# Token tiles by feature through VectorE's block transposes and DRAM in a one-core DiT block

## The chip, the core and the metric

The kernel runs on one core of one Trainium2 chip. The metric is the device time in microseconds of one execution; lower is better. The core has a matrix engine (TensorE, PE in the profile, with its weight loads as PEld), VectorE (DVE), ScalarE (ACT), GpSimd (POOL), and SyncE (SP), which here only issues DMAs. Each engine works through its own queue in order; the engines wait for one another by semaphores.

## The reference

One block of a diffusion transformer in float32: B = 2 sequences of N = 2048 tokens, C = 576 features, H = 16 heads of 36, an MLP of 2304. Cut to what matters:

```python
mod = silu(c) @ w_ada + b_ada          # 6 rows of C per sequence
sh1, sc1, g1, sh2, sc2, g2 = split(mod, 6)
xn = ln(x, 1e-6) * (1 + sc1) + sh1
q, k, v = split(xn @ w_qkv + b_qkv)    # (B, N, H, 36) each
q, k = ln(q, 1e-5, qn_g, qn_b), ln(k, 1e-5, kn_g, kn_b)
o = softmax(q @ k.T / 6) @ v
x = x + g1 * (o @ w_proj + b_proj)
xn2 = ln(x, 1e-6) * (1 + sc2) + sh2
out = x + g2 * (gelu(xn2 @ w1 + b1) @ w2 + b2)
```

A matmul on PE needs the features, over which it sums, on the partitions. Tokens are normed with a token on each partition, because the mean and variance are over its features. So every tile of 128 tokens has to be turned from tokens on partitions to features on partitions, twice in the block: ahead of the q/k/v products and ahead of the MLP's first product. The modulation by `sc` and `sh` is applied after turning, where scale and shift are one number for each partition.

## The kernel before

The branch that runs is `block_of_small`. It does everything in one program with these stages, in this order: the adaptive rows; for each sequence, the q/k/v products of 16 token tiles (`inputs`), attention (`attend`) and the projection (`outputs`); then the MLP over all tokens.

576 features are four chunks of 128 and a last one of 64. A turned tile has the last 64 features twice, on partitions 0 to 63 and 64 to 127: `rows_normed` copies columns 512:576 behind the row (L280), so that a fifth PE transpose of 128 columns yields both copies.

*q/k/v.* In `inputs`, a tile has three products (q, k, v) of 576 outputs, each as two halves of 288 columns. `whole` (L400) does the four full chunks as float32 matmuls; `halved` (L411) does the last 64 features as a matmul on half of the array's rows, partitions 0 to 63 for one half of the columns and 64 to 127 for the other. Turning is by `transposed`: four PE transposes at L357, one at L358, into PSUM. ACT then modulates from PSUM to SBUF (`modulated`, L365, five instructions). The turned tile of t+1 is made during tile t, between its q and k products; the norm of t+2 follows. VectorE evicts the products with their bias (`biased`), centres the heads of q and k, and turned heads go through nine PE transposes (L938). For the first two tiles of all, x is loaded ahead, and the first tile of batch 0 is turned with the adaptive rows.

*Projection.* `outputs(b)` does o times w_proj with the residual in groups of four tiles. VectorE multiplies the product by the gate (L1183) and adds x (L1190); POOL's queue loads the residual's rows (L1178) and stores them (L1191). A dictionary `between` hangs further work on certain tiles: in batch 0's projection the first tile of batch 1; in batch 1's the norm, transposes and modulation of the MLP's first five tiles, and the eight `weight_sums` on VectorE, of which four split the MLP's last 64 weight rows, wr, into float32r parts (`weight_parts`, L394 and L395, with L1358).

*MLP.* The first product is a scheme of seven products for four blocks of weights and tokens, in 72 jobs: eight blocks of 512 tokens, nine jobs to a block. Float32 matmuls at L1445 do the 512 full features, and float32r matmuls at L1459 the last 64. [...] the rows are split into a rounded part and what is left, and their products are summed. `last_modulated` (L382, L383) makes two ACT outputs of the last features, a float32r one in `parts` and a float32 one in `tail`; POOL subtracts them (L384). `gelu_stored` evicts each job: ACT copies one part out of PSUM (L1471), VectorE does four sums (L1472 to L1479), ACT the gelus (L1483), SP's queue the stores. `ahead(job)` prepares the next block's four tiles: x is loaded by POOL's queue three jobs early, normed one job early, turned by four PE transposes one job later and by the fifth two jobs later (L1505), and modulated (L1515).

*What sets the order.* PE's order follows the program text. VectorE's order is written by hand (`manual_schedule`) in `inputs`, in `attend`, and from batch 1's projection through the MLP; the other queues are ordered by a planner, so a queue can take an instruction ahead of another where the text has it later. A tile pool with `bufs=1` has one buffer for a name: the next writer waits for the last reader.

## Time and profile before

| | us |
|---|---|
| median of 3 runs | 3216.81 (3216.06 to 3217.01) |
| profiled execution | 3216.58 |
| its span in the profile | 3214.8 |
| PE busy | 3192.7 |
| ACT busy | 1509.1 |
| VectorE busy | 1459.6 |
| POOL busy | 369.1 |
| q/k/v of batch 0, of batch 1 | about 18.9 to 258, 1109.7 to 1347 |
| attention of batch 0, of batch 1 | to 1037.7, to 2120.85 |
| projection of batch 0, of batch 1 | to 1109.7, to 2199.98 |
| MLP's first product, second product | to 2719.28, to 3213 |

The mean granted clock of TensorE is 0.999 of full speed. The stages are read from PE's timeline in microseconds from the span's start; each is given by its end where it begins at the end of the one before. The profiled execution is 1.8 us longer than its span, which covers the core's instructions alone.

In a group's line, "out<-in" names the tiles that an instruction writes and reads, then come its shape, its count, its busy time and the mean length of one in nanoseconds, and last the idle time of its engine just before it with what ended that. Matmuls overlap one another, so a mean length is longer than what one matmul takes of PE. A float32 matmul has two records, a float32r matmul one.

### The profile page before, as it was taken

What the parts mean: (1) busy time and instruction counts of PE and PEld (TensorE: products, weight loads), DVE (VectorE), ACT (ScalarE), POOL (GpSimd) and SP (SyncE); (2) the same over time, 40 slices, a digit from 0 to 9 for tenths busy, and PEclk for the clock granted to TensorE, in tenths of its full rate; (3) what the DMA queues carried; (4) which work ended last, traced back from release to release, by engine and by line L of the source; (5) the groups of instructions that cost most, each with busy time, mean ns of one, the idle gap of its engine ahead of it and who ended that gap; (6) DMA issues with size and microseconds to landing.
All of it is one profiled execution on the core that took longest, in us unless ns stands there. A gap on an engine that the chain in (4) does not pass through costs nothing.

```text
span 3214.8 us, 47053 instructions
## 1 busy us (share of the span) xinstructions
PE 3192.7 (99%) x18143; PEld 1904.6 (59%) x18143; DVE 1459.6 (45%) x2137; ACT 1509.1 (47%) x2984; POOL 369.1 (11%) x464
## 2 busy tenths in 40 slices
PE   8999999999999999999999999999999999999999
PEld 6774333333333777633333333358888888777777
DVE  4674333333333367633333333345555444455454
ACT  2335666666666033466666666633555552000000
POOL 2111000112110111200001111011000000111111
PEclk9999999999999999999999999999999999999999
DMA  4102212223221401121222223144322223333321
GB/s 132 30 26 68 75 33 69 64 72 86 71 81 34 145 23 31 30 54 44 48 47 67 65 69 75 44 160 166 121 88 91 95 80 128 136 133 111 118 103 38
DMA packets 129172, 252.86 MB, mean 79 GB/s; under 512 B 22947, under 2 KB 68460, under 8 KB 126828
## 3 DMA queue, kind: packets, MB, share of 16 engines
q1 hardware_dynamic: 105428, 181.78, 18.6%
q0 software_dynamic: 22640, 66.23, 7.4%
q8 instruction: 145, 2.38, 0.3%
q10 hardware_dynamic: 872, 1.77, 0.2%
q14 instruction: 87, 0.71, 0.1%
HBM read 135.11 MB, written 66.35 MB: 63 GB/s over the span
## 4 chain that ended last, share of the span: by engine, by line
PE 98%; DMA 1%; DVE 0%; SPq 0%; issue 0%; ACT 0%; POOL 0%; DVEq 0%; POOLq 0%
PE b L1086 28%; PE b L1073 19%; PE s L1610 15%; PE s L400 15%; PE m L1445 12%; PE m L1459 2%; PE s L411 2%; PE one L1445 2%; PE s L938 1%; PE s L357 0%; PE t L1505 0%; DMA wq<-in_w_qkv_dram 0%; DMA x_dram<-x 0%; PE b L192 0%; PE b L938 0%
## 5 line engine op out<-in xcount | busy, mean ns | idle before, releaser
L1077 ACT ACTIVATE pt<-b 128x512 f32<-128x512 f32 x2048 | 1057.7, 610 | 485.3 <-PE b L1086 272.2
L1086 PE MATMUL b<-pt,vt 128*64 128x512 f32 x4096 | 935.0, 599 | 0.0
L1086 PEld LDWEIGHTS b<-pt,vt 128*64 128x64 f32 x4096 | 272.0, 136 | 581.8 <-issue 439.2
L1073 PE MATMUL b<-qm,km 32*128 32x512 f32 x4096 | 566.9, 614 | 0.2 <-DMA km<-qo 0.2
L1134 DVE TENSOR_TENSOR ot<-b,ot 128x512 f32<-128x512 f32 x192 | 132.8, 692 | 652.9 <-PE b L1086 652.5
L1073 PE MATMUL b<-qe,ke 16*128 16x512 f32 x2048 | 423.1, 790 | 0.0
L400 PE MATMUL s<-wq,xnt 128*128 128x288 f32 x1536 | 391.4, 409 | 1.2 <-ACT xnt L882 0.8
L1610 PE MATMUL s<-ws,as 128*128 128x288 f32 x1440 | 351.8, 406 | 0.0
L1073 PEld LDWEIGHTS b<-qm,km 32*128 32x128 f32 x4096 | 191.8, 185 | 269.1 <-ACT pt L1077 207.0
L400 PEld LDWEIGHTS s<-wq,xnt 128*128 128x128 f32 x1536 | 285.1, 190 | 85.4 <-issue 13.5
L1610 PEld LDWEIGHTS s<-ws,as 128*128 128x128 f32 x1440 | 274.1, 190 | 75.1
L1105 DVE RECIPROCAL den<-den 128x512 f32<-128x512 f32 x64 | 213.6, 3337 | 10.8 <-DMA den<-den_dram 10.8
L1445 PE MATMUL m<-s,wb 128*128 128x256 f32 x864 | 210.1, 380 | 0.2 <-DVE s L1415 0.2
L1445 PE MATMUL m<-xnt,wb 128*128 128x256 f32 x864 | 210.2, 379 | 0.0
L1132 DVE COPY ot<-b 128x512 f32<-128x512 f32 x64 | 44.3, 692 | 334.7 <-PE b L1086 334.7
L1445 PEld LDWEIGHTS m<-s,wb 128*128 128x128 f32 x864 | 164.4, 190 | 22.5 <-DVE s L1415 0.6
L1073 PEld LDWEIGHTS b<-qe,ke 16*128 16x128 f32 x2048 | 108.3, 184 | 114.2 <-issue 112.8
L1445 PEld LDWEIGHTS m<-xnt,wb 128*128 128x128 f32 x864 | 159.1, 190 | 18.7
L1472 DVE TENSOR_TENSOR cs<-m,cs 128x512 f32<-128x512 f32 x72 | 49.8, 691 | 215.8 <-PE m L1459 207.1
L1610 PE MATMUL s<-ws,hidden 128*128 128x288 f32 x576 | 142.3, 406 | 0.0
L1588 DVE TENSOR_TENSOR as<-hidden 128x1152 f32<-128x1152 f32 x80 | 139.2, 1803 | 0.0
L400 PE MATMUL s<-wp,qo 128*128 128x288 f32 x512 | 127.8, 410 | 0.0
(182 smaller groups left out, 2573.9 us busy)
## 6 DMA issues: line engine op xcount, KB each, us to landing
gelu<-cs SPq DMA_DIRECT2D x144, 256.0 KB
hidden<-gelu SPq DMA_DIRECT2D x16, 2304.0 KB
den<-den_dram SPq DMA_DIRECT2D x128, 128.0 KB
x_dram<-kr POOLq DMA_DIRECT2D x48, 288.0 KB, 2.8
qm<-qo SPq DMA_DIRECT2D x192, 64.0 KB
kr<-in_x_dram POOLq DMA_DIRECT2D x32, 288.0 KB, 3.8
xr<-x_dram SPq DMA_DIRECT2D x32, 288.0 KB
out_dram<-y POOLq DMA_DIRECT2D x30, 288.0 KB, 3.8
```

What stands on the lines that cost most here:

```text
L400: nc.tensor.matmul(outs[a], stationary(k, a), moving(k, a), start=(first and k == 0), stop=(not first and k == FULL - 1),)
L411: nc.tensor.matmul(outs[a], stationary(FULL, a)[r], moving(FULL, a)[r], start=first, stop=not first)
L1073: nc.tensor.matmul(ps, k[r, keys], q[r, :], start=first, stop=not first)
L1077: nc.scalar.activation(pt[:, h, :], banks[2 * c + h], AF.Exp, scale=SCALE)
L1086: nc.tensor.matmul(acc[64 * h : 64 * h + 64, :], vt[:, v0 : v0 + 64], pt[:, h, :], start=pt is pts[0][0], stop=pt is pts[-1][0],)
L1105: nc.vector.reciprocal(den, den)
L1134: nc.vector.tensor_tensor(ot, acc, ot, ALU.add)
L1445: nc.tensor.matmul(out_m[m], wb[:, slot[m], k, f * P : (f + 1) * P], moving[m](k), start=k == 0 and m in (1, 2, 5, 6), stop=k == 1 and m == 1,
L1459: nc.tensor.matmul(out_m[m], wr[w][:, f * P : (f + 1) * P], a[:, i, t * PAIR : (t + 1) * PAIR], start=False, stop=i == 1 and m != 2,)
L1472: nc.vector.tensor_tensor(cs[:, 0:5:4, :], two(1), cs[:, 4:5, :].to_broadcast([P, 2, PAIR]), ALU.add)
L1588: nc.vector.tensor_tensor(stationary[m], x_, y_, op)
L1610: nc.tensor.matmul(ms[m], stationary[m][:, f, :], ws[m][:, f, :], start=(f == 0), stop=(f == HF - 1))
```

## The change

Turned tiles no longer come from PE. VectorE transposes the normed tile in blocks of 32x32 into a tile `squares` (one buffer). Four DMAs write it to DRAM with runs of 32 numbers, 128 bytes, so that DRAM holds the tile with features as rows (`tile_turned`). Three DMAs read it back with features on partitions: the four full chunks into `xnt`, the last 64 features twice into `tail` (`turned_loaded`). ACT modulates in place (`turned_modulated`). The first tile and, as `second_by_feature`, the second tile of batch 0 are still turned by PE.

The q/k/v products no longer use `halved`: the last 64 features of a tile are split into float32r parts as the MLP's are, and so are the last 64 rows of w_qkv, by `weight_parts` on VectorE, which come through the tile `bq` before the bias is loaded into it. For each half of the columns, two float32r matmuls take the place of the halved one, for 12 instead of 6 of a tile's matmuls.

The splitting of the MLP's last weight rows goes from VectorE to POOL (`last_parts`). In the MLP x is loaded four jobs ahead, normed and written two jobs ahead, read back at the job and modulated at the next. The DMAs go by SP's queue in `inputs` and in the MLP, and by ACT's in the two projections.

```diff
@@ -266,7 +266,7 @@
-    def rows_normed(pool, xt):
+    def rows_normed(pool, xt, repeated=True):
@@ -277,7 +277,8 @@
-        nc.scalar.copy(xt[:, C:], xt[:, 512:576])
+        if repeated:
+            nc.scalar.copy(xt[:, C:], xt[:, 512:576])
@@ -373,6 +374,14 @@
+    def part_tiles(pool, cols, **bufs):
+        return (
+            pool.tile([P, FULL, cols], F32, name="xnt", **bufs),
+            pool.tile([P, 2, cols], F32R, name="xnt4", **bufs),
+            pool.tile([P, P], F32, name="tail", bufs=1),
+        )
     def affine(which, k, b):
@@ -385,14 +394,17 @@
     def modulated_parts(dst, cols, t4, t1, which, b):
-        last_modulated(dst, cols, t1, which, b)
...
-    def weight_parts(dst, src):
-        nc.vector.tensor_copy(dst[0:64], src)
-        nc.vector.tensor_tensor(dst[64:128], src, dst[0:64].bitcast(F32), ALU.subtract)
+        last_modulated(dst, cols, t1, which, b)
+    def weight_parts(dst, src, subtract=None):
+        if subtract is None:
+            nc.vector.tensor_copy(dst[0:64], src)
+        else:
+            subtract.tensor_copy(dst[0:64], src)
+        (subtract or nc.vector).tensor_tensor(dst[64:128], src, dst[0:64].bitcast(F32), ALU.subtract)
     def whole(outs, stationary, moving, first):
@@ -748,13 +760,13 @@
-        def token_tiles(count):
+        def token_tiles(count, width=C):
             pool, close = opened("xs", side="right")
-            more = [pool.tile([P, C + 64], F32, name=f"xt{i}") for i in range(count - 1)]
+            more = [pool.tile([P, width], F32, name=f"xt{i}") for i in range(count - 1)]
...
-        close_xs = token_tiles(5)
+        close_xs = token_tiles(3, C + 64)
@@ -846,13 +858,14 @@
         def input_weights(then=lambda t: None):
...
-            wq4 = pool.tile([P, 3, HALF], F32, name="wq4")
+            wq4 = pool.tile([P, 3 * C], F32R, name="wq4")
...
-                    last_chunk(wq4, w_qkv, 3, HALF)
+                    nc.sync.dma_start(out=bq[0:64, :], in_=w_qkv[512:576, :])
+                    weight_parts(wq4, bq[0:64, :])
@@ -868,27 +881,61 @@
         def tile_normed(xt):
...
-        def input_rows(b, t, queue):
-            return tile_normed(tile_loaded(x[b, t * P : (t + 1) * P, :], queue))
-        def input_by_feature(b, rows, apart=False):
-            xnt = xs["pool"].tile([P, NKC, P], F32, name="xnt", bufs=2)
-            modulated(xnt, rows, 0, b, apart)
+        SQ = 32
+        def tile_turned(xt, queue):
+            rows_normed(xs["pool"], xt, repeated=False)
+            squares = xs["pool"].tile([P, C], F32, name="squares", bufs=1)
+            nc.vector.transpose(squares, xt[:, :C])
+            xs["count"] = xs.get("count", 0) + 1
+            turned = dram.tile([C, P], F32, name=f"turned{xs['count']}")
+            by_square = turned.rearrange("(k d) (g j) -> g d k j", d=SQ, j=SQ)
+            for g in range(P // SQ):
+                queue.dma_start(
+                    out=by_square[g], in_=squares[g * SQ : (g + 1) * SQ, :].rearrange("p (k j) -> p k j", j=SQ)
+                )
+            return turned
+        def turned_loaded(dst, cols, turned, queue):
+            full, _, tail = dst
+            queue.dma_start(out=full[:, :, cols], in_=turned[0:512, :].rearrange("(k p) n -> p k n", p=P))
+            for r0 in (0, 64):
+                queue.dma_start(out=tail[r0 : r0 + 64, :], in_=turned[512:576, :])
+        def turned_modulated(dst, cols, which, b):
+            full, _, tail = dst
+            for k in range(FULL):
+                part = full[:, k, cols]
+                nc.scalar.activation(part, part, AF.Identity, **affine(which, k, b))
+            last_modulated(dst, cols, tail, which, b)
+        def input_turned(b, t, queue):
+            return tile_turned(tile_loaded(x[b, t * P : (t + 1) * P, :], queue), queue)
+        def input_loaded(turned, queue):
+            xnt = part_tiles(xs["pool"], P, bufs=2)
+            turned_loaded(xnt, slice(0, P), turned, queue)
...
+        def input_modulated(b, xnt):
+            turned_modulated(xnt, slice(0, P), 0, b)
+            return xnt
+        def second_by_feature(rows):
+            xnt = part_tiles(xs["pool"], P, bufs=2)
+            t4, t1 = transposed(*rows, True)
+            modulated_parts(xnt, slice(0, P), t4, t1[:, :P], 0, 0)
+            return xnt
         def first_modulated():
...
+            xnt = part_tiles(xs["pool"], P, bufs=2)
+            modulated_parts(xnt, slice(0, P), x_first[:, :512], x_first[:, 512:], 0, 0)
...
-        def inputs(b, weights, work, xnt, loaded):
+        def inputs(b, weights, work, xnt, rows, loaded):
@@ -965,18 +1012,20 @@
             def next_rows(t):
-                return tile_normed(loaded.pop(0)) if loaded else input_rows(b, t, nc.sync)
+                return tile_turned(loaded.pop(0), nc.sync) if loaded else input_turned(b, t, nc.sync)
             def product(w, xnt):
...
...
+                full, parts, _ = xnt
+                for a in range(2):
+                    f = slice(w * C + a * HALF, w * C + (a + 1) * HALF)
+                    out_a = ps[:, a, :HALF]
+                    for k in range(FULL):
+                        nc.tensor.matmul(out_a, full[:, k, :], wq[:, k, f], start=k == 0, stop=False)
+                    for i in range(2):
+                        nc.tensor.matmul(out_a, parts[:, i, :], wq4[:, f], start=False, stop=i == 1)
+                return ps
             def biased(w, ps, t, both):
@@ -991,34 +1040,28 @@
-            rows = next_rows(1)
+            if b == 0:
+                rows = tile_normed(loaded.pop(0))
...
-                q, q_parts = product(0, xnt)
-                whole(*q_parts, True)
-                behind = b == t == 0
-                if behind:
-                    k, k_parts = product(1, xnt)
-                    whole(*k_parts, True)
-                ahead = input_by_feature(b, rows, t in ((0, 9), (0, 1))[b])
+                turning = b == t == 0
+                if not turning:
+                    ahead = input_loaded(rows, nc.sync)
+                q = product(0, xnt)
+                k = product(1, xnt)
+                if turning:
+                    ahead = second_by_feature(rows)
+                else:
+                    input_modulated(b, ahead)
                 rows = next_rows(t + 2)
-                if not behind:
-                    k, k_parts = product(1, xnt)
-                    whole(*k_parts, True)
-                v, v_parts = product(2, xnt)
-                halved(*q_parts, False)
-                halved(*k_parts, False)
-                halved(*v_parts, True)
...
-                whole(*v_parts, False)
+                v = product(2, xnt)
@@ -1028,16 +1071,17 @@
+                if t + 1 < NT:
+                    ahead = input_loaded(rows, nc.sync)
                 for w in range(3):
-                    ps, parts = product(w, xnt)
-                    two_products(*parts, 3 * t + w)
+                    ps = product(w, xnt)
...
-                            ahead = input_by_feature(b, rows)
+                            input_modulated(b, ahead)
@@ -1294,11 +1338,13 @@
-                    9: [lambda: opening.update(rows=input_rows(b + 1, 0, nc.scalar))],
-                    14: [lambda: opening.update(xnt=input_by_feature(b + 1, opening["rows"]))],
+                    6: [lambda: opening.update(rows=input_turned(b + 1, 0, nc.scalar))],
+                    8: [lambda: opening.update(xnt=input_loaded(opening["rows"], nc.scalar))],
+                    10: [lambda: opening.update(rows=input_turned(b + 1, 1, nc.scalar))],
+                    12: [lambda: input_modulated(b + 1, opening["xnt"])],
...
-                xnt = opening["xnt"]
+                xnt, rows = opening["xnt"], opening["rows"]
@@ -1352,11 +1398,14 @@
+        left, right = last_rows[:, 0], last_rows[:, 1]
+        last_parts = [
+            lambda: weight_parts(wr[0], left, nc.gpsimd),
+            lambda: weight_parts(wr[1], right, nc.gpsimd),
+            lambda: nc.gpsimd.tensor_tensor(right, right, left, ALU.subtract),
+            lambda: weight_parts(wr[2], right, nc.gpsimd),
+        ]
         weight_sums = [
-            lambda: weight_parts(wr[0], last_rows[:, 0]),
-            lambda: weight_parts(wr[1], last_rows[:, 1]),
-            lambda: nc.vector.tensor_tensor(last_rows[:, 1], last_rows[:, 1], last_rows[:, 0], ALU.subtract),
-            lambda: weight_parts(wr[2], last_rows[:, 1]),
@@ -1368,22 +1417,23 @@
-        def block_modulated(to, i, turned, b):
-            t4, t1 = turned
-            modulated_parts(to, slice(i * P, (i + 1) * P), t4, t1[:, :P], 2, b)
...
-            between.setdefault(2 * j + 6, []).append(
-                lambda j=j, n=n, i=i: block_modulated(xnts[n], i, transposed(*first[j]), 0)
+            cols = slice(i * P, (i + 1) * P)
+            between.setdefault(2 * j + 6, []).append(lambda n=n, cols=cols: turned_modulated(xnts[n], cols, 2, 0))
+            between.setdefault(2 * j + 1, []).append(
+                lambda j=j, n=n, i=i: first.update({j: mlp_loaded(n, i, nc.scalar)})
...
-                lambda j=j, n=n, i=i: first.update({j: mlp_loaded(n, i, nc.scalar)})
+                lambda j=j: first.update({j: tile_turned(first[j], nc.scalar)})
             )
-            between.setdefault(2 * j + 5, []).append(lambda j=j: first.update({j: tile_normed(first[j])}))
-        for i, t in enumerate((6, 7, 8, 9, 10, 11, 12, 14)):
+            between.setdefault(2 * j + 4, []).append(
+                lambda j=j, n=n, cols=cols: turned_loaded(xnts[n], cols, first[j], nc.scalar)
+            )
+        for i, t in enumerate((6, 8, 10, 12)):
             between.setdefault(t, []).append(weight_sums[i])
+            between.setdefault(t + 1, []).append(last_parts[i])
@@ -1493,32 +1542,18 @@
-            if todo := at(-3):
+            if todo := at(-4):
                 rows_ahead[todo] = mlp_loaded(*todo, nc.gpsimd)
-            if todo := at(-1):
-                rows_ahead[todo] = tile_normed(rows_ahead[todo])
-            for offset, chunks in ((1, range(FULL)), (2, (FULL,))):
+            if todo := at(-2):
+                rows_ahead[todo] = tile_turned(rows_ahead[todo], nc.sync)
+            for offset in (0, 1):
...
-                    src, tail = rows_ahead[todo] if offset == 1 else rows_ahead.pop(todo)
...
+                    cols = slice(i * P, (i + 1) * P)
+                    if offset == 0:
+                        turned_loaded(xnts[m % 2], cols, rows_ahead.pop(todo), nc.sync)
+                    else:
+                        turned_modulated(xnts[m % 2], cols, 2, m // NBLK)
```

More of the change, by code (lines that the diff above doesn't have):

```diff
@@ L877, in input_by_feature @@
             return xnt
         def first_modulated():
-            xnt = xs["pool"].tile([P, NKC, P], F32, name="xnt", bufs=2)
-            for k in range(NKC):
-                nc.scalar.activation(
-                    xnt[:, k, :],
-                    x_first[:, k * P : (k + 1) * P],
-                    AF.Identity,
-                    bias=mod[:, 0, k, 0:1],
-                    scale=mod[:, 1, k, 0:1],
-                )
+            xnt = part_tiles(xs["pool"], P, bufs=2)
+            modulated_parts(xnt, slice(0, P), x_first[:, :512], x_first[:, 512:], 0, 0)
@@ L967, in next_rows @@
             def next_rows(t):
-                return tile_normed(loaded.pop(0)) if loaded else input_rows(b, t, nc.sync)
+                return tile_turned(loaded.pop(0), nc.sync) if loaded else input_turned(b, t, nc.sync)
             def product(w, xnt):
                 ps = s_tile()
-                return ps, (
-                    [ps[:, a, :HALF] for a in range(2)],
-                    lambda k, a: xnt[:, k, :],
-                    lambda k, a: (
-                        wq[:, k, w * C + a * HALF : w * C + (a + 1) * HALF] if k < FULL else wq4[:, w, :]
-                    ),
-                )
+                full, parts, _ = xnt
[7 more added lines that the diff above has]
+                return ps
             def biased(w, ps, t, both):
@@ L1230, in block_of_small @@
         xnt = first_modulated()
-        loaded = []
+        rows, loaded = None, []
         weights, close_weights = input_weights(
@@ L1237, in block_of_small @@
             with tc.manual_schedule(engines={mybir.EngineType.DVE}):
-                last_inputs = inputs(b, weights, work, xnt, loaded)
+                last_inputs = inputs(b, weights, work, xnt, rows, loaded)
             close_weights()
@@ L1409, in block_of_small @@
         ps_m1 = banks.tile([P, 2, PAIR], F32, name="one")
-        ps_t = banks.tile([P, 512], F32, name="t")
         def token_sums(n):
@@ L1494, in at @@
                 return (m + 1, g // 2) if there else None
-            if todo := at(-3):
+            if todo := at(-4):
                 rows_ahead[todo] = mlp_loaded(*todo, nc.gpsimd)
-            if todo := at(-1):
-                rows_ahead[todo] = tile_normed(rows_ahead[todo])
-            for offset, chunks in ((1, range(FULL)), (2, (FULL,))):
+            if todo := at(-2):
+                rows_ahead[todo] = tile_turned(rows_ahead[todo], nc.sync)
+            for offset in (0, 1):
                 if todo := at(offset):
                     m, i = todo
-                    src, tail = rows_ahead[todo] if offset == 1 else rows_ahead.pop(todo)
-                    for k in chunks:
-                        nc.tensor.transpose(
-                            ps_t[:, k % FULL * P : (k % FULL + 1) * P],
-                            src[:, k * P : (k + 1) * P] if k < FULL else tail,
-                            ident,
-                        )
-                    block = xnts[m % 2]
-                    if offset == 2:
-                        last_modulated(block, slice(i * P, (i + 1) * P), ps_t[:, :P], 2, m // NBLK)
-                        continue
-                    for k in chunks:
-                        nc.scalar.activation(
-                            block[0][:, k, i * P : (i + 1) * P],
-                            ps_t[:, k * P : (k + 1) * P],
-                            AF.Identity,
-                            bias=mod[:, 2, k, m // NBLK : m // NBLK + 1],
-                            scale=mod[:, 3, k, m // NBLK : m // NBLK + 1],
-                        )
+                    cols = slice(i * P, (i + 1) * P)
[3 more added lines that the diff above has]
+                        turned_modulated(xnts[m % 2], cols, 2, m // NBLK)
         for m, k, n in ((2, 0, 0), (5, 1, 1), (3, 0, 1), (4, 1, 0)):
```

## The prediction

> **What bounds the kernel now.** I read the page's first and fourth parts, then PE's groups by shape, then PE's timeline over one q/k/v tile and over the second projection. On the page:
>
> ```profile
> PE 3192.7 (99%) x18143; PEld 1904.6 (59%) x18143; DVE 1459.6 (45%) x2137; ACT 1509.1 (47%) x2984; POOL 369.1 (11%) x464
> PE 98%; DMA 1%; DVE 0%; SPq 0%; issue 0%; ACT 0%; POOL 0%; DVEq 0%; POOLq 0%
> ```
>
> PE is 99% of the span and 98% of the chain, the other engines under half. An instruction taken from PE is worth its whole slot; one put elsewhere costs only if PE comes to wait for it. PE's groups that the change touches (out<-in, shapes, count | busy us, mean ns | idle before):
>
> ```profile
> L400 PE MATMUL s<-wq,xnt 128*128 128x288 f32 x1536 | 391.4, 409 | 1.2 <-ACT xnt L882 0.8 <-DMA wq<-in_w_qkv_dram 0.4
> L1459 PE MATMUL m<-parts,wr 128*128 128x256 f32 x576 | 91.0, 301 | 0.0
> L411 PE MATMUL s<-wq,xnt 64*128 64x288 f32 x384 | 56.0, 422 | 0.3 <-ACT xnt L365 0.3
> L357 PE MATMUL s<-ident,xt 128*128 128x128 f32 x116 | 18.1, 280 | 3.3 <-DVE product L1183 3.3
> L1505 PE MATMUL t<-ident,xt 128*128 128x128 f32 x90 | 15.7, 273 | 0.0
> ```
>
> The means overlap, so I price by start-to-start, from the timeline (start, length, count):
>
> ```profile
> 103.48 4.15 PE L400 MATMUL s<-wq,xnt 128*128 128x288 f32 x16
> 107.46 1.15 PE L938 MATMUL s<-ident,both 128*128 128x128 f32 x9
> 108.44 4.05 PE L400 MATMUL s<-wq,xnt 128*128 128x288 f32 x16
> 112.33 0.60 PE L357 MATMUL s<-ident,xt 128*128 128x128 f32 x4
> 112.76 0.27 PE L358 MATMUL s<-ident,xt 128*128 128x128 f32 x1
> 112.87 4.05 PE L400 MATMUL s<-wq,xnt 128*128 128x288 f32 x16
> 116.85 1.73 PE L411 MATMUL s<-wq,xnt 64*128 64x288 f32 x12
> 118.50 0.51 PE L400 MATMUL s<-wq,xnt 128*128 128x288 f32 x1
> ```
>
> From 103.48 to 118.50 a tile takes 15.02 us: 48 whole records at about 0.2425 (11.64), nine transposes 0.98, five of tokens 0.54 (0.109 each), and the twelve halved records what remains, 1.86. In the MLP eight float32r records take 0.955 (a job of 7.00 less its float32 records at 0.216 a record), 0.119 for 256 columns.
>
> [...] two records of 0.2425 are 0.485 a matmul, against one record of 0.119 x 288/256 = 0.134[...]. [...] No transpose of VectorE's is in this trace. [...] The trace has packets of 144 bytes at 12 to 15 ns, so 128 bytes cost little here. [...] Here a 128x1152 multiply takes POOL 2.126 us, and VectorE's 64x1152 subtract 1.351: ratio 1.57.
>
> **Part by part, PE.** *Loops of q/k/v.* Five transposes (0.54) and 1.86 of halved records go; twelve float32r records of 0.121 to 0.134 come, 1.45 to 1.61. Each full loop gains 0.79 to 0.95, I take 0.88; it becomes 14.14 us. Batch 0 has 13 such loops (11.4), and two last tiles that halve each product apart, which gains 1.8 by the same records. Its start loses: bq's rows and VectorE's conversion of 64x1728 (0.743 x 1.5 + 1.351 x 1.5 = 3.1) come before the first float32r product, so the first tile ends near 35.2 for 34.2: +1.0 (0 to 4). Batch 0: -12.2. Batch 1: 14 loops (12.3), its first tile's transposes (0.5) and the last two (1.8): -14.6. *Projection of batch 1.* 25 transposes, -2.7. *MLP.* 27 tiles by 0.545, -14.7. Sum: -44.2.
>
> The second projection also holds a wait that its transposes meet:
>
> ```profile
> 2165.58 2.21 PE L411 MATMUL s<-wp,qo 64*128 64x288 f32 x16
> 2171.10 1.12 PE L357 MATMUL s<-ident,xt 128*128 128x128 f32 x4 [3.32 <-DVE product L1183]
> 2172.23 9.01 PE L400 MATMUL s<-wp,qo 128*128 128x288 f32 x32
> ```
>
> PE waits 3.3 there, and the next instructions run longer than their like, start to start: 1.13 against 0.54, and 8.84 against 32 x 0.2425 = 7.76, 1.7 together. That is 5 us that go if VectorE is early: -49.2 in all.
>
> **Part by part, the other engines.** *VectorE* loses nothing in PE's cover: its busy time in that tile,
>
> ```profile
> 103.55:118.57 15.02, 15.02 (x75) 11.57 (x75) 9.95 (x19) 5.15 (x13) 2.13 (x1) 1.00 0.15 33
> ```
>
> is 9.95 of 15.02 (third figure after PE and weight loads). A block transpose of 576 columns is bounded by a pass of tensor_scalar, 0.58[...]; I take 0.66. 10.6 of 14.14 fits[...]. Without the cover, 62 tiles (30 in q/k/v, 32 in the MLP) at 0.66 would be 41 us. *ACT* reads SBUF instead of PSUM, one or two more operations of 0.46 a tile, one copy of 0.24 less; 5.6 of 14.1. *POOL* gets a 0.487 subtract a tile. *DMAs*: each turned tile adds 4 writes and 3 reads, about 0.55 us of issue each (POOL's loads show 0.55), so 3.9 us on SP, and 2304 packets of 128 bytes: at 14 ns over 16 engines 2.0 us, then about 3 to land. From VectorE's transpose to the modulated tile: 0.66 + 2.2 + 3 + 1.7 + 3 + 2.5 = 13 us; transposed in the middle of loop t, needed at the start of loop t+2, it has about 21. Only loops in which 11 DMAs of qm or km stand ahead of the read on SP come near: 1 us in all (0 to 6). At the end of batch 0's inputs, ACT's in-order queue takes batch 1's first tiles' DMAs and the wait of each amid the evictions and first exponentials: +3 (1 to 5).
>
> *Where a stall goes: second projection.* POOL's seven operations for the MLP rows (three copies, four 64x1152 tensor_tensors) are at 2.1 each at most, 12 to 15 us, where VectorE took 7.7; they stand in one row on POOL. Behind them wait the stores and loads of x1 and the first tile's subtraction of L393. The tile of 128 "tail" columns has one buffer, so ACT's next load of it (ACT issues these DMAs itself) waits for that subtraction. Behind this load on ACT is the square root of tile 3, and behind that on VectorE, in its order by hand, the norm of tile 3, ahead of the eviction that frees PE's slots. Starting the POOL row near 2152 to 2155, when its loads before are let go:
>
> ```profile
> 2151.93 0.54 POOL L1178 DMA_DIRECT2D x<-x_dram  x1 [8.87 <-DMA x_dram<-x]
> ```
>
> it ends near 2167, the subtraction follows at 2170 to 2179, the root at 2176 to 2188; PE, which would begin that group of tiles at about 2168, waits some 12 us (0 to 20). If the chain is short, the wait of before goes and none comes.
>
> *MLP.* SP carries 4 stores, 4 writes and 3 reads for each pair of jobs, 11 x 0.55 = 6 of 14; ACT's tile waits for the read, with copies and gelus behind it. In the built order a tile's read mostly stands ahead of the next tile's writes, so writes, read and landing (about 9 us) run beside ACT's 8.7 of work, under the 14 of a pair: +3 (0 to 12).
>
> Sum: 3216.6 - 49.2 + 1 + 3 + 12 + 3 = 3186. The profiled execution took 3216.58 us, 1.8 above its span of 3214.8 and 0.2 from the median 3216.81, so the sum holds for the median.
>
> **Rivals.**
> *All cover holds:* no stall in the projection or the tail: 3216.6 - 49.2 = 3167; for it, PE's 3192.7 busy and every other engine under half. Against it, single-buffered tail and ACT's queue.
> *Reads become a bound in part:* packets or SP's order delay a read in most tiles by a us or less on PE, 3200 to 3210. For it: 5.8 us from issue to landing of x<-x_dram in the busy projection; against: DMA busy 15% in the q/k/v tile.
> *float32r gains nothing:* if leaving float32 cost a switch as the halved ones do (four turns, 0.1 each), a loop gains 0.4 less, 28 x 0.4 = 11: 3197. L1459's 0.955 for eight in between float32 speaks against.
> *Slower, the MLP's closed loop:* ACT's modulation waits for a read that SP issues behind the next tile's writes, those wait for VectorE's transpose, it for ACT's root behind the gelus. In series: ACT 8.7, norm and transpose 1.4, a group of VectorE's sums in the way 3.2, writes 2.2, read 0.6 and landing 3.1: up to 19.2 a tile. Nine jobs of 7.00 carry four tiles, 15.75 each. From (3223.2 - 3186)/28 = 1.3 above that, 17.1 us a tile, the kernel is slower than before; at 19.2, 3186 + 97 = 3283. The order found in most blocks breaks this loop.
>
> **How the numbers follow.** The measurement can tell 0.2%, 6.4 us: faster below 3210.4, slower above 3223.2. Chances: my case with a stall in the projection (3175 to 3200) 0.54; all cover holds (below 3175) 0.19; reads in part or float32r without gain (to 3210) 0.13; the closed loop, or several late reads, 0.14, of which 0.05 end within the bound and 0.09 slower. Faster 0.86. For 8 in 10 the range goes from the clean case, 3166, to 3208.
>
> **What would show it.** Right: a q/k/v loop near 14.1, transposes of L1505 gone and jobs near 7.0 each, L411 with wq gone, VectorE's transposes near 0.66. In the second projection PE waits about 12 us for VectorE, whose norm waits for ACT, whose load waits for POOL. Wrong: VectorE's transpose over 2.5 us, 128-byte packets over 60 ns (7 us more per tile eat the loop's slack), or PE waiting in the MLP for L1521 or the copies: then the time lies higher.

## The result

The changed kernel takes 3209.27 us (median of 12 runs, 3205.0 to 3212.09); the kernel before, 3216.91 (12 runs, 3214.91 to 3219.19). The ratio is 0.9975, 95% interval 0.9966 to 0.9984: faster by 0.25%. The forecast was 3186 with a range of 3166 to 3208. The sign was right; a quarter of the gain came, and the time lies just outside the range.

The twelve runs of the changed kernel lie 7.1 us apart, and their mean granted clock goes with the time: 0.996 in the fastest, 0.994 in the slowest, where the kernel before has 0.999 in its profiled run.

The profiled execution of the changed kernel has a span of 3209.8 us; it took 3212.09 us, the longest of the twelve, so its stages together show 2.8 us more than the median. Its page, parts 1 and 4:

```profile
PE 3164.1 (99%) x17833; PEld 1897.9 (59%) x17833; DVE 1506.7 (47%) x2196; ACT 1521.8 (47%) x2954; POOL 398.9 (12%) x503
PE 94%; DMA 2%; DVE 1%; SPq 1%; POOL 1%; issue 0%; ACT 0%; ACTq 0%; DVEq 0%; POOLq 0%
```

PE has 28.6 us less work by its records, and the span fell by 5.0. PE's share of the chain went from 98 to 94%: other things now end waits on the way to the end. The view of PE's waits (engine, line, released by: us in all, times, longest) names them:

```profile
PE s L412 <- DVE product L1227: 15.6, 2, 12.3
PE s L306 <- DVE x_first L279: 8.5, 1, 8.5
PE b L985 <- ACT pt L1121: 4.0, 1, 4.0
PE s L313 <- ACT xnt L398: 1.7, 1, 1.7
PE s L1027 <- DVE wq L407: 1.5, 1, 1.5
```

Each line says which matmuls of PE waited and which engine's instruction let them go. The second is the start of the program and was there before (8.3). The first is batch 1's projection, the third the opening of batch 0's attention, the last two the start of q/k/v. Stage by stage, from PE's first instruction of each stage in the two profiles (the forecast's gains include its own waits):

| stage | before | after | gained | forecast |
|---|---|---|---|---|
| start and q/k/v, batch 0 | 258.65 | 252.75 | 5.9 | 12.2 |
| attention, batch 0 | 779.0 | 792.0 | -13.0 | -3 |
| projection, batch 0 | 72.0 | 71.5 | 0.5 | 0 |
| q/k/v, batch 1 | 238.4 | 227.1 | 11.3 | 13.6 |
| attention, batch 1 | 772.8 | 772.9 | -0.2 | 0 |
| projection, batch 1 | 79.1 | 92.5 | -13.4 | -4.3 |
| MLP, first product | 519.1 | 505.4 | 13.8 | 11.7 |
| MLP, second product | 495.7 | 495.6 | 0.1 | 0 |

Where the work is steady, the change does what was forecast. In two stages without steady work it loses 26.4, and in the start of q/k/v it gains half of what was forecast.

### The profile page after: what moved, and what is told of

Its sections match the earlier page's. It is cut to its first block, busy times and chain, and to the rows that moved or that the text cites. A ratio compares the mean times of both kernels' runs of the same rounds, so it can differ in the third digit from the quotient of the medians.

```text
span 3209.8 us, 47255 instructions
## 1 busy us (share of the span) xinstructions
PE 3164.1 (99%) x17833; PEld 1897.9 (59%) x17833; DVE 1506.7 (47%) x2196; ACT 1521.8 (47%) x2954; POOL 398.9 (12%) x503
## 4 chain that ended last, share of the span: by engine, by line
PE 94%; DMA 2%; DVE 1%; SPq 1%; POOL 1%; issue 0%; ACT 0%; ACTq 0%; DVEq 0%; POOLq 0%
PE b L1130 29%; PE b L1117 19%; PE s L1645 15%; PE m L1494 11%; PE s L1025 10%; PE s L412 2%; PE m L1508 2%; PE one L1494 2%; PE s L1027 1%; PE s L985 1%; DMA x_dram<-x 1%; DMA bq<-in_w_qkv_dram 0%; PE s L423 0%; DMA turned<-squares 0%; DMA xnt<-turned 0%
## 5 line engine op out<-in xcount | busy, mean ns | idle before, releaser
L1130 PE MATMUL b<-pt,vt 128*64 128x512 f32 x4096 | 937.4, 600 | 0.0
L1130 PEld LDWEIGHTS b<-pt,vt 128*64 128x64 f32 x4096 | 272.4, 137 | 584.4 <-issue 442.3
L1025 PE MATMUL s<-wq,xnt 128*128 128x288 f32 x1536 | 406.3, 408 | 1.4 <-ACT xnt L391 0.8
L1532 ACT ACTIVATE cs<-cs,b_sb 128x512 f32<-128x512 f32 x144 | 101.7, 720 | 116.9 <-DVE cs L1527 113.4
L412 PE MATMUL s<-wp,qo 128*128 128x288 f32 x512 | 131.1, 417 | 16.4 <-DVE product L1227 15.6
```

The source lines that it names most:

```text
L412: nc.tensor.matmul(outs[a], stationary(k, a), moving(k, a), start=(first and k == 0), stop=(not first and k == FULL - 1),)
L1025: nc.tensor.matmul(out_a, full[:, k, :], wq[:, k, f], start=k == 0, stop=False)
L1130: nc.tensor.matmul(acc[64 * h : 64 * h + 64, :], vt[:, v0 : v0 + 64], pt[:, h, :], start=pt is pts[0][0], stop=pt is pts[-1][0],)
L1532: nc.scalar.activation(part, part, AF.Gelu, bias=b1_sb[:, g : g + 1])
```

## The steady stages

PE's timeline of the changed kernel over one q/k/v tile (start, length, count):

```profile
65.36 1.14 PE L985 MATMUL s<-ident,both 128*128 128x128 f32 x9
66.34 2.11 PE L1025 MATMUL s<-wq,xnt 128*128 128x288 f32 x8
68.07 0.64 PE L1027 MATMUL s<-wq,xnt 128*128 128x288 f32 x2
68.56 2.10 PE L1025 MATMUL s<-wq,xnt 128*128 128x288 f32 x8
...
79.58 1.14 PE L985 MATMUL s<-ident,both 128*128 128x128 f32 x9
```

From 65.36 to 79.58 it is 14.22 us, for 15.02 before and 14.14 forecast. Half a product takes 2.205 us, start to start (66.34 to 68.56, and the same on average over the tile). If its four float32 matmuls still take 0.485 each, as in the timeline of before, its two float32r matmuls take 0.1325 each by this estimate. VectorE's new transpose:

```profile
L890 DVE STREAM_TRANSPOSE squares<-xt 128x576 f32<-128x576 f32 x41 | 31.9, 778 | 7.2 <-DMA turned<-squares 5.9
```

It takes 0.778 us for 0.66 assumed, and the loop covers it. The loop covers the DMAs too, but for one late read in each batch (1.45 us over two loops). A job of the MLP is 7.00 us but for two at its start, its transposes gone.

## The attention's opening: a wait and a slow clock

The windows of the changed kernel there (stretch, length, then busy time of PE, weight loads, VectorE, ScalarE and POOL, granted clock of PE as a share of full speed, DMA share, GB/s):

```profile
252.75:257.25 4.50, 3.76 (x25) 2.20 (x24) 2.01 (x4) 2.36 (x6) 3.19 (x3) 1.00 0.44 103
257.25:260.75 3.50, 0.00 (x0) 0.00 (x0) 0.00 (x0) 2.47 (x4) 1.58 (x4) 1.00 0.86 169
260.75:274.45 13.70, 13.27 (x41) 6.67 (x43) 2.52 (x7) 8.59 (x18) 0.46 (x1) 0.50 0.21 47
274.45:281.00 6.55, 6.55 (x43) 2.70 (x41) 2.38 (x6) 2.58 (x5) 2.93 (x7) 1.00 0.25 50
```

PE stands from 257.2 to 261.2, and then works for 13 us with a granted clock of 0.50. The wait costs 4.0, the clock by estimate half of 13.27, 6.6. ScalarE's timeline says what PE waits for:

```profile
255.04 0.49 ACT L392 ACTIVATE tail<-tail,mod 128x128 f32<-128x128 f32 x1
258.25 0.88 ACT L912 ACTIVATE xnt<-xnt,mod 128x128 f32<-128x128 f32 x2 [2.72 <-DMA xnt<-turned]
259.15 1.28 ACT L1121 ACT_TABLE_LOAD   x1
260.44 2.06 ACT L1121 ACTIVATE pt<-b 128x512 f32<-128x512 f32 x4
```

The planner took the first two tiles of batch 1, which are wanted 850 us later, into the end of batch 0's q/k/v. ScalarE modulates them, and stands 2.72 us for the second one's read, in front of the first exponential. That comes at 260.44, as in the kernel before (260.27), though PE began the scores 5.9 us sooner.

**Held back.** The first two tiles of batch 1 wait for the end of batch 0's attention: an element of the tile to load is written from the last chunk of `qo`, so the load has to wait for that chunk.

```diff
+                def held(b, t, queue):
+                    nc.vector.tensor_copy(xs["tiles"][0][0:1, 0:1], qo[0:1, NKC - 1, N - 1 : N])
+                    return input_turned(b, t, queue)
...
-                    6: [lambda: opening.update(rows=input_turned(b + 1, 0, nc.scalar))],
+                    6: [lambda: opening.update(rows=held(b + 1, 0, nc.scalar))],
...
-                    10: [lambda: opening.update(rows=input_turned(b + 1, 1, nc.scalar))],
+                    10: [lambda: opening.update(rows=held(b + 1, 1, nc.scalar))],
```

> The changed kernel with the first two tiles of batch 1 held back until the end of batch 0's attention, so that ScalarE has none of their work ahead of the first exponentials. Clock theory: PE's wait of 4.0 us there goes and with it the half clock of 13.7 us that follows; attention of batch 0 takes 779 to 781 us for 792, the time is near 3197. Bare-wait theory, as the forecast priced it: only the waits go, 4.7 us, the time is 3204. The tiles' work lies then in batch 0's projection; if PE waits there, up to 5 us come back.

Measured: 3196.87 us, ratio to before 0.9939 (0.9922 to 0.9955), 12.4 under the changed kernel. Attention takes 780.4, for 779.0 before and 792.0 after the change. The wait on L985 is gone, and the same stretch has its clock:

```profile
254.00:258.00 4.00, 4.00 (x33) 2.62 (x29) 2.52 (x7) 3.74 (x9) 1.46 (x3) 1.00 0.55 91
258.00:272.00 14.00, 14.00 (x87) 5.31 (x83) 4.54 (x11) 7.78 (x16) 3.13 (x7) 1.00 0.22 38
```

PE has 87 records in 14.0 us, where the changed kernel had 41 in 13.7. The waits alone, 4.7 us, would have left the time near 3204.6. In batch 0's projection, where the tiles are turned now, nothing is lost (71.5 us).

**The same wait put into the kernel before.** Useless activations ahead of the first exponential, 14 in one kernel, 5 in the other:

```diff
+                        if b == p == qb == g == c == 0 and k0 == 0:
+                            for _ in range(14):
+                                nc.scalar.activation(pt[:, 0, :], kr[:, 0, 0:BLK], AF.Identity)
```

> The kernel before with 14 useless activations of 128x512 on ScalarE (0.51 us each, 7.2 us) ahead of the first exponential of batch 0's attention. PE has some 1 to 2 us of slack there, so it waits 5 to 6 us. Clock theory: the granted clock then falls to 0.5 [...] as after the change, up to 13.7; attention of batch 0 takes 787 to 793 us for 779, the time is 3225 to 3230. Bare-wait theory: 784 to 785, 3222 to 3223.

> The kernel before with 5 useless activations (2.6 to 3.2 us) ahead of the first exponential of batch 0's attention, for 14 in the long one, where PE waited 4.1 us, the clock was 0.5 for 13.7 us and the time rose 13. Clock theory: PE waits 1 to 2 us, [...]the clock stays 1.0, and the time rises by 0 to 3 us: 3217 to 3220. If any wait halves the clock, it rises by 8 or more.

Measured with 14, of which ScalarE did 7 before the first exponential and 7 among the next: a PE wait of 4.1 us, attention 790.9 for 779.0, and 3230.12 in one run. With 5: a wait of 2.7, attention 786.0, 3222.65 in one run. The windows of the short one:

```profile
262.64:265.45 2.81, 0.06 (x3) 0.09 (x2) 0.00 (x0) 2.75 (x5) 2.41 (x5) 0.99 0.56 112
265.45:275.65 10.20, 10.20 (x37) 6.12 (x39) 2.52 (x7) 5.39 (x11) 0.00 (x0) 0.50 0.12 15
```

So a wait of 2.7 us cost 7.0, one of 4.1 cost 11.9, in a kernel without the change: the slow clock follows from the wait. The short one was meant to make a wait of 1 to 2 us and leave the clock alone. The wait came out longer, and the clock fell. Not every wait of this length does it. In one of these two runs PE waits 2.88 us in batch 1's projection, 3.32 in the profile of the kernel before. There the next 32 records of the product took 9.01 us; here they keep their speed:

```profile
2178.86 0.66 PE L357 MATMUL s<-ident,xt 128*128 128x128 f32 x4 [2.88 <-DVE product L1186]
2179.46 7.93 PE L400 MATMUL s<-wp,qo 128*128 128x288 f32 x32
```

Other profiles of this stage, most of kernels further down, show both. Behind a wait of 2.15 us the next 32 records took 9.65 us for 8.03 (most of w1 not loaded, rows on VectorE), behind 2.83 they took 9.72 (POOL's splits undone) and behind 3.33 again 9.72 (the changed kernel); behind waits of 2.00 (tiles held back) and 2.40 us (rows of w_qkv first) they took 8.03. So the length of a wait of 2 to 3 us does not tell whether the clock falls; what else decides was not shown.

In the changed kernel's profile the clock is 0.50 for 6.8 us at the start, for 13.7 at the attention's opening, and in the second projection for 13.7, beginning within the long wait, and for 3.4 in the work behind the other. At the attention's opening the length differs between kernels that have the same program there. Some 8 us after the end of the wait of 4.0 us the first 16 records of L1130 took 6.10 us in the changed kernel, and 3.65 with POOL's splits undone and with w1 later (both below), which is their length at clock 1.00 (at 2103.34 in the changed kernel). What sets that length was not shown either.

## The second projection: more than one chain

In the changed kernel PE waits 12.28 us at 2164.60, then 3.33 at 2188.14:

```profile
2164.60 10.11 PE L412 MATMUL s<-wp,qo 128*128 128x288 f32 x32 [12.28 <-DVE product L1227]
2174.64 2.21 PE L423 MATMUL s<-wp,qo 64*128 64x288 f32 x16
2176.78 8.03 PE L412 MATMUL s<-wp,qo 128*128 128x288 f32 x32
2188.14 9.72 PE L412 MATMUL s<-wp,qo 128*128 128x288 f32 x32 [3.33 <-DVE product L1227]
```

The two groups after the waits are 2.1 and 1.7 us longer than the 8.03 of their like: the granted clock was 0.50 up to 2168.85, and from 2189.33 to 2192.74. VectorE in front of the long wait, until the product at 2163.80 that lets PE go on:

```profile
2150.58 0.16 DVE L278 RECIPROCAL rstd<-std 128x1 f32<-128x1 f32 x1 [14.36 <-ACT std L276]
2150.78 0.58 DVE L279 TENSOR_SCALAR x_first<-x_first,mv,rstd 128x576 f32<-128x576 f32 x1
2158.39 0.78 DVE L890 STREAM_TRANSPOSE squares<-x_first 128x576 f32<-128x576 f32 x1 [7.04 <-DMA turned<-squares]
2159.10 4.78 DVE L1234 TENSOR_TENSOR x<-x,product 128x576 f32<-128x576 f32 x2
```

It stands 14.4 us for a square root, and 7.0 for `squares`, which the first tile's writes still hold. Then two adds take 4.78 us, for 1.42 elsewhere; POOL's splits run from 2151.5 to 2166.4, and the last section returns to that. The root came late since ScalarE issues those writes, and was held at it:

```profile
2135.32 14.89 ACTq L895 DMA_DIRECT2D turned<-squares  x2
2150.25 0.29 ACT L276 ACTIVATE std<-mv,eps 128x1 f32<-128x1 f32 x1 [17.58 <-issue]
```

Two issues took 14.89 us, where a write's issue takes 0.5 to 0.6 elsewhere. The DMA engines are full in this time, with w1's 4.7 MB and x1's rows:

```profile
2138.00:2154.00 16.00, 14.32 (x66) 10.43 (x64) 0.74 (x2) 0.29 (x1) 3.87 (x6) 1.00 1.04 410
```

They were in the kernel before too (407 GB/s from 2142 to 2158), but nothing on the way to PE's slots then passed through them in this stage's beginning. The second wait has the links of the forecast's chain: the tail load waits for POOL, the root of tile 3 for the load, the norm for the root.

```profile
2163.34 3.02 POOL L407 TENSOR_TENSOR wr<-last_rows,wr 64x1152 fp32r<-64x1152 f32 x1
2174.74 0.54 POOL L1222 DMA_DIRECT2D x<-x_dram  x1 [3.19 <-DMA x_dram<-x]
2177.19 0.54 POOL L1222 DMA_DIRECT2D x<-x_dram  x1 [1.90 <-DMA x_dram<-x]
2177.79 0.45 POOL L393 TENSOR_TENSOR parts<-tail,parts 128x128 fp32r<-128x128 f32 x1
2178.27 1.10 ACTq L905 DMA_DIRECT2D tail<-turned  x2
2184.21 0.28 ACT L276 ACTIVATE std<-mv,eps 128x1 f32<-128x1 f32 x1
2184.52 0.16 DVE L278 RECIPROCAL rstd<-std 128x1 f32<-128x1 f32 x1 [6.74 <-ACT std L276]
```

POOL's splits end at 2166.4. Up to the subtraction at 2177.8 its queue holds stores and loads of x1, and four waits for stores to land, 7.1 us together. Two theories, then: S, POOL's splits, as forecast; D, the full DMA engines.

**The stage as before.** PE turns the first five tiles again, with `tile_normed`, `transposed` and `modulated_parts` at their old places, and the rows are split on VectorE.

> The changed kernel with the whole of batch 1's projection as before: the MLP's first five tiles turned by PE, the rows split on VectorE. Both theories: the projection is 79 us again for 92.4, with the 3.3 us wait of before; the MLP begins near 2195.6, the time is 3196 (3194 to 3199). If it stays over 3203, the loss in this stage is from neither POOL nor the writes.

Measured: 3197.19 us, ratio 0.9936 (0.992 to 0.9953), the stage 80.5 us. The loss is of this stage's part of the change. A wait like that of before, 3.4 us, is back, and the 32 records of the product behind it took 10.25 us for 7.93.

**POOL's splits undone.**

```diff
-            lambda: weight_parts(wr[0], left, nc.gpsimd),
+            lambda: weight_parts(wr[0], left),
...
-        for i, t in enumerate((6, 8, 10, 12)):
+        for i, t in enumerate((6, 7, 8, 9, 10, 11, 12, 14)):
...
```

> The changed kernel with the MLP's last weight rows split on VectorE, at the places of before, and nothing else undone. Theory S, the forecast's: POOL's row of seven operations holds the tail load on ACT, the root and the norm behind it; then both waits of PE in batch 1's projection (12.3 and 3.3 us) go but for some 4 us, and the MLP begins near 2196 for 2208.8, the time is near 3196. Theory D: the 12.3 us are the 128-byte writes of the first tile, queued among the 4.7 MB of w1 rows while the DMA engines are full, with one buffer of squares behind which VectorE stands; then that wait stays within 2 us, only the 3.3 and its slow clock (5 us together) go, and the time is 3204 to 3207.

Measured: 3211.0 us, ratio 0.9978 (0.9971 to 0.9986), the stage 93.1 us, with waits of 9.2, 2.8 and 2.1. Theory S fell: the edit gains nothing in all. Theory D's 3204 to 3207 wasn't met either, nor its bound that the long wait stays within 2 us. The long wait is 3.1 us shorter, because without POOL's splits the two adds in front of it are quick:

```profile
2156.01 1.38 DVE L1234 TENSOR_TENSOR x<-x,product 128x576 f32<-128x576 f32 x2
```

So the splits do make a part of the long wait, but VectorE's own splits and the new wait of 2.1 take it back.

**Two buffers of squares**, in turn:

```diff
-            squares = xs["pool"].tile([P, C], F32, name="squares", bufs=1)
+            squares = xs["more"].pop(0) if xs.get("more") else xs["pool"].tile([P, C], F32, name="squares", bufs=1)
...
-        outputs(B - 1, wp, between, [scratch.tile([P, C], F32, name=f"x1_{i}") for i in range(9)])
+        more = [scratch.tile([P, C], F32, name=f"squares{i}") for i in range(2)]
+        xs["more"] = [more[i % 2] for i in range(TPB + 1)]
+        outputs(B - 1, wp, between, [scratch.tile([P, C], F32, name=f"x1_{i}") for i in range(7)])
```

> The changed kernel with two buffers of squares in turn in batch 1's projection (and seven for nine of its x1 tiles, to make room). Theory D: VectorE no longer stands 7.0 us at its second transpose for the first tile's writes, but ScalarE is still held 11.5 us at the issue of the last of these writes, so that the norm ends near 2151 as before; PE's long wait is 4 to 6 us for 12.3, the time 3200 to 3204. If ScalarE's hold is what counts alone, the wait stays over 9 and the time at 3207 to 3210.

Measured: 3217.13 us, ratio 0.9998 (0.9989 to 1.0007). PE's long wait became two of 2.4 and 4.7 us, but a later one grew from 3.3 to 7.1, and PE waits 1.9 and 3.2 us for VectorE's sums of tokens at the MLP's start. The time saved was lost behind. The group of tiles after the later wait begins 72.4 us into the stage, 71.8 in the changed kernel: the second chain runs beside the first, and taking from the first only makes PE wait longer for the second. The edit is not a clean one. With seven tiles of x1 for nine a load comes late, and VectorE stands for it in front of the wait of 2.4:

```profile
2139.58 0.76 DVE L1234 TENSOR_TENSOR x<-x,product 128x576 f32<-128x576 f32 x1 [12.34 <-DMA x<-x_dram]
```

**w1 later.** The four blocks' loads are held until the first two tiles are turned.

```diff
+        def rows_loaded(i):
+            k, f = divmod(i, 2)
+            nc.vector.tensor_copy(wb[0:1, i, 0, 0:1], eps6[0:1])
...
+        for i in (0, 1, 3, 2):
+            between.setdefault(6, []).append(lambda i=i: rows_loaded(i))
+        for i, t in enumerate((9, 10, 12, 14)):
+            between.setdefault(t, []).append(weight_sums[i])
...
```

> The changed kernel with w1's four blocks (4.7 MB) loaded after the first two tiles of batch 1's projection are turned, and the sums of them later; nothing else. Theory D: the first tile's writes find free DMA engines, are issued in 2.3 us and land in some 3; PE's wait of 12.3 falls below 4, without the slow clock after it; the MLP begins near 2197 (2195 to 2202, its sums may come late), the time is 3195 to 3203. If the writes are slow of themselves, because of their 128-byte packets, the wait stays over 9 and the time over 3206.

Measured: 3208.36 us, ratio 0.9971 (0.996 to 0.9981). The wait of 12.3 is gone, and the first tile's four writes are issued in 4.2 us for 15.9: so w1's load on the DMA engines made that wait, and not the packets' size. The wait at the second chain's group is 15.8 us now, for 3.3, and the group begins 69.9 us into the stage:

```profile
2184.85 9.78 PE L412 MATMUL s<-wp,qo 128*128 128x288 f32 x32 [15.80 <-DVE product L1227]
```

It is the same chain: POOL's loads of x1 wait for stores to land (6.46 us, while w1 is loaded), its subtraction stands behind them, and ScalarE's tail load behind that. With the splits on VectorE besides:

> The changed kernel with w1's blocks loaded later, as in the run before, where the long wait moved to 15.8 us behind the tail load, and with the rows split on VectorE instead of POOL. If POOL's splits made that second wait, it shrinks to under 5, the MLP begins near 2196 and the time is 3196 to 3200. If POOL is held by its own x1 loads, which wait for stores to land while w1 is loaded, the wait stays over 9 and the time is 3203 to 3210.

Measured: 3212.9 us, ratio 0.9987 (0.998 to 0.9993), the stage 94.9 us. The wait of 15.8 is gone, and one of 11.8 came at an earlier group, by another way: ScalarE stands 15.6 us for the second tile's writes, which lie among w1's loads now. So this run does not part POOL's splits from the DMA engines.

**Most of w1 not loaded.**

```diff
+            nc.gpsimd.memset(wb[:, i], 0.0)
             nc.sync.dma_start(
-                out=wb[:, i],
...
+                out=wb[:, i, :, 0 : MH // 8],
...
```

> The changed kernel with only an eighth of the columns of w1's four blocks loaded (0.6 for 4.7 MB); GpSimd sets the blocks to zero before, at the stage's start, so the MLP's result is not the reference's, while every other instruction stays. If the full DMA engines are what holds batch 1's projection, both waits of PE there shrink: 12.3 to under 3, and the second, 3.3, to under 3; the MLP begins near 2194 to 2198 for 2208.9, the time is 3194 to 3199. If POOL's row of splits and ScalarE's queue hold it without them, a wait of 6 us or more stays and the time is over 3201.

> The run with an eighth of w1's columns loaded (blocks set to zero before, so the MLP's result is not the reference's), and the rows split on VectorE besides. In that run the projection took 86.1 us for 92.5 after the change and 79.1 before, with waits of 2.9 and 3.8 us left. If full DMA engines and POOL's splits together make the loss, the waits fall under 2.5 each, the clock stays and the projection takes 76 to 80 us: 3193 to 3198. If the round trip of tail load, root and norm holds it of itself, a wait of 3 us or more stays, and the stage takes 83 to 87: 3200 to 3204.

Measured: 3203.03 us, ratio 0.9955 (0.9939 to 0.9972), with waits of 2.9 and 3.8 and a stage of 86.1; with the rows on VectorE 3197.68, ratio 0.994 (0.9923 to 0.9957), waits of 2.6 and 2.1 and 82.8. In both most of w1 is zero, so the result is not the reference's. So of the 92.5 us w1's loads make 6.4, and without them POOL's splits make 3.3, by one profile each; setting the zeros takes POOL 7.9 us at the stage's start in both. With w1 loaded, undoing the splits gained nothing. 82.8 lies between what the two theories expected, 76 to 80 and 83 to 87. PE's work in the stage is about 71.5 us; short waits, slow clock and the gaps round them make the other 11, and their causes stay open.

## The start

> The changed kernel with the last 64 rows of w_qkv loaded and split ahead of the other rows. The first q/k/v tile ends at 38.9 us for 34.2 before. The wait for VectorE's parts (1.5 us) goes, and if the split is done by 20 us [...]its clock isn't halved from 21.9 to 28.7 (3.4 us); the tile ends at 34.5 to 37.5, the time is 3205 to 3208. If the other rows come later by as much, nothing is gained: 3209.

Measured: 3210.6 us, ratio 0.9978 (0.997 to 0.9987): no gain. The loads of w_qkv's last rows went ahead of the loop, but VectorE's cast came at 21.03 us for 22.19, since its order by hand puts it behind the adaptive rows. PE still waited 1.6 us for it, then 1.5 for the second tile, whose rows came later, and before that 2.2 for rows of w_ada, 0.2 in the changed kernel. The first tile ends at 38.0 us. In this profile the clock is not halved at the start at all, where the changed kernel's was 0.50 from 21.87 to 28.69; but this execution is the fastest of its fourteen, 5 us under the median, so it does not stand for the others.

## Both repairs together

> Two repairs in one: the first tiles of batch 1 held back (3196.9 alone) and batch 1's projection by PE as before (3197.2 alone); the rest is the changed kernel. The two stages don't touch, so 3209.3 - 12.4 - 12.1 = 3184.8 (3183 to 3188), faster than both kernels.

Measured: 3187.35 us, ratio 0.9905 (0.9889 to 0.9922). It is faster than both kernels, within the 3183 to 3188 expected, and its gain over the kernel before, 30 us, is nearly four times that of the change: the q/k/v loops and the MLP of the changed kernel, with its two losing stages repaired. PE's waits, after that of the program's start:

```profile
PE s L358 <- DVE product L1227: 3.6, 1, 3.6
PE s L1027 <- DVE wq L407: 1.5, 1, 1.5
```

## Why the prediction was wrong

The mechanism in the steady stages was right. A q/k/v loop gained 0.81 for 0.88: float32r matmuls cost 0.1325, near the upper of the two prices given, 0.134; the lower, 0.121, was the author's estimate, and no trace showed it. Over 27 loops that is 1.9 us. In each batch one late read also cost 1.45 us over two loops, where 1 us in all was put down, 1.9 more. The MLP's 14.7 came nearly whole; its closed loop, the rival that was to make the kernel slower, didn't close. The packets of 128 bytes took 13 ns (the median of 142,848), as priced.

The term that failed first is "+3 (1 to 5)" for the end of batch 0's inputs; 13.0 were lost. The wait was named with its cause, ScalarE's work and the read in front of the first exponential, and its size, 4.0, lies inside. What it sets off was left out: 6.6 us of half clock. Of the rest, 1.8 lie between the scores, 0.7 of it a wait for VectorE's eviction of v; the run with the tiles held back has most of this too, 780.4 for 779.0. The view of before had shown the slow clock. The prediction took 1.7 us of slow instructions after a 3.3 us wait from the timeline, and counted them as something that goes, not as something that can come with every new wait.

The second is "PE waits some 12 us" in batch 1's projection: 15.6 of waits, 4 of clock and about 1 of gaps, for 12. The long wait, 12.3, isn't the one that was forecast, and its nearness to 12 is chance: it was the issue of the first tile's writes, held at DMA engines full with w1, then the wait for their landing, then adds slowed beside POOL's splits. The forecast's chain is there, with its links in the order named, and POOL's seven operations took 14.9 us for 12 to 15, though each tensor_tensor took 2.6 to 3.0 for "at most" 2.1. It shows only 3.3 us because PE comes to it late; with the first wait gone PE waited 15.8 for it. Only a part of its length is the splits': without them that group of tiles begins 68.3 us into the stage for 71.8, and behind them POOL's queue waits 7.1 us for stores of x1. So the step that failed is the price of the DMAs in this stage, and with it the wait that the sum did not have. The page's own slices (160 and 166 GB/s there, the highest of all), and POOL's 8.87 us of standing for x1's store in the very line that the prediction quotes, said that a round trip through DRAM isn't 3 us in this stage. The sum priced it at 3 everywhere.

The third is "+1.0 (0 to 4)" for the start, and it is less sure. In the two profiles it is 4.7: the split on VectorE was costed at 3.1 and took 3.0, but the first product also begins 1.9 later and PE's clock is 0.50 round the wait, from 21.87 to 28.69. Nine other profiles have the same start, and there the first tile ends at 36.1 to 40.1 us, in five of them below 37.7, where this one has 38.9; the two runs on the kernel before have 35.5 and 36.1 for 34.2, with 9.69 us for the first 32 records of the product in both, for 8.03 elsewhere. By these the start lost some 2 us, inside the range, and the rest of 4.7 is chance of these two executions.

The stages missed the forecast's gains by 25.2 us in all. These three terms are 22.8 of it (10.0, 9.1 and 3.7) and the loops 3.8; the MLP, 2.1 better, goes the other way, and rests of 0.7 remain.

## What to carry to other kernels

When work is taken off the busiest engine, price the steady loops by start-to-start times, and then look at each seam between stages by itself: what each in-order queue has ahead of the first instruction of the next stage, and how full the DMA engines are in that stretch. Where the profile shows the clock falling after a PE wait, a new wait is to be priced at its length and a slow clock that may come behind it: in these runs 32 records in the projection took 1.1 to 2.8 us longer behind some waits and kept their speed behind others (2.00, 2.40 and 2.88 us), and at the attention's opening waits of 2.7 and 4.1 us cost 7.0 and 11.9 in all. When two chains run side by side, taking one away shows the other at its full length. A planner that fills a queue with work wanted much later can be held back by a write that depends on what is to come first; one such line was worth 12.4 us here.

## What was not expected of the hardware

A PE wait of 2.7 us cost 7.0 and one of 4.1 cost 11.9 in the attention's opening, with the clock at 0.50 for 10.2 and 13.7 us, while one of 2.88 in the projection cost no clock at all. While POOL did its splits, VectorE's instructions were slower: an add of 128x576 (L1234) took 2.39 us for 0.71 outside, and the sum of 128x2304 (L1409) 3.64 for 2.54. With POOL's splits undone the adds were back at 0.69; what in POOL's work slowed them was not shown. DMAs issued by ScalarE, with 128-byte packets, held it for 14.9 us at two issues when the DMA engines were full (share 1.04, 410 GB/s); at 2179.41, with a share of 0.61, four such issues took 2.28 us.
